# An attention stage whose key weights are stored once and sorted on the chip: one graph kernel, one change

## The chip, the cores and the metric

The kernel runs on one core of a Trainium2 chip. The core has a matrix engine (TensorE, "PE", whose weight loads the profile lists apart as "PEld"), a vector engine (VectorE, "DVE"), a scalar engine with lookup functions (ScalarE, "ACT"), a general engine (GpSimd, "POOL") and a queue processor (SyncE, "SP"), each with its own in-order list of instructions, and sixteen DMA engines between main memory (HBM) and on-chip memory (SBUF). Matrix products land in PSUM, eight banks of 512 numbers on each of 128 partitions. The metric is the device time of one execution in microseconds. Before the change it is 12,053.6 us, the median of three runs (12,050.65 to 12,054.63).

## The reference

The input is `x` (3,327 nodes by 128) and a dense matrix `adj` (3,327 by 3,327). Four layers follow each other, each of the form `x = x + layer(relu(layernorm(x)), adj)`. Only layer 0 matters here; it takes nearly all the time. It is an attention with an unusual reshape:

```
q = (x @ Wq.T).reshape(d, n, h)      # d = 128 "heads", n = 3327 nodes, h = 8 elements
k = (x @ Wk.T).reshape(d, n, h)
v = (x @ Wv.T).reshape(d, n, h)
a = einsum('dnh,dmh->dnm', q, k) * scale + adj + adj
a = softmax(a, axis=2)
out = einsum('dnm,dmh->dnh', a, v).reshape(n, h * d)
return out @ Wo.T
```

So there are 128 heads of only 8 elements, and for each of them a full 3,327 by 3,327 table of exponentials, 1.4 thousand million in all. Layers 1 to 3 multiply `adj` with a matrix of 128 columns and do work per node.

## The kernel before

**Preparing (the first 390 us).** `x` is normalized and projected. For q and for k, the projection of a pair of node tiles is split into a high part rounded to the matrix engine's fast format (`F32R`) and the remainder: ACT copies PSUM to the high part (L364), DVE subtracts it (L365), ACT squares it (L366), POOL sums the squares (L368), and SP stores both halves (L371) to `qS_d` and `kS_d` in HBM. A bound on the scores is formed from the norms. A second path (the functions `whole` and `part_of`), taken only where that bound is large, is skipped with this input.

**The main stage.** The work is cut into chunks `c` of 476 queries (7), groups `g` of four heads (32), and pairs `q` of key tiles (13); a key tile is 128 keys, spaced 13 apart. One (c, g, q) is a unit; there are 2,912, taken in that order. In a unit, for two key tiles r = 0, 1:

- `seed` (DVE, L612) copies the pair's tiles of transposed `adj` (already less a bound per query, L560) into PSUM.
- `scores` (PE, L618) adds the products of one head's k and q on top, in rows 64r to 64r+63 of the array, a separate bank for each r. The 64 rows hold the high and low parts of the new head's k and q, and of the previous head's with q negated, so that each head's table is made out of the previous head's.
- `exps` (ACT, L630) takes exp of two banks at a time, 952 numbers on each partition.
- `values` (PE, L638) multiplies them with v and a column of ones into one bank `po`, four heads in four column strips.

For a group's end `store` copies `po` (DVE, L650) and POOL issues four small stores (L654).

**Loads.** All loads of the next group are issued by SP when unit q = 1 of the present group comes up (`load_qk`): per head j and half r, two transfers of 16 rows of k into `KT` (L525) and three of q into `QS` (L527, L529), 40 in all; then two of v (L543). `KT`, `QS` and `VA` have two buffers each. `KT` holds k as it lies in HBM, so the weights of one key tile are every 13th column (`q::NQ`, 52 bytes apart). At q = 4 POOL negates q (L537), spreads v (L549) and touches the loaded tile (`all_here`, L553); the group's first score waits for that.

**Order.** All engines' orders in this stage are written out by hand: a loop over time slots `i`, four per unit, emits the exponentials of unit u and head j at slot 4u + 3j, the scores one or two slots ahead, and the values 11 and 13 slots behind. Side work is put at units by `plan(u, f)`. Between the groups a square of `adj` for the next chunk is read and turned by `plan_squares`; the maximum of its rows ("a row's bound") goes through HBM: `gather` (four stores, L299), `back` (one load into `four`, L304), `finish` (two small DVE operations, L308 and L309, and a store, L310), at 12, 16 and 20 units after the load of the second half.

**The rest (from 10,937 us).** The output product and layers 1 to 3.

Of the kernel before, what the change touches and what calls it, by code (L numbers as in the profile page):

```python
# [10 lines left out]
F32 = mybir.dt.float32  # L11
# [3 lines left out]
F32R = mybir.dt.float32r  # L15
# [7 lines left out]
P = 128  # L23
N = 3327
D = 128
H = 8
# [59 lines left out]
def gnn_kernel(ctx: ExitStack, tc: tile.TileContext, x, adj, Wq, Wk, Wv, Wo, embed, layer,  # L86
# [13 lines left out]
    qS_d = dram.tile([2, H, GP], F32, name="qS_d")  # L100
    kS_d = dram.tile([2, H, GP], F32, name="kS_d")
    oT_d = dram.tile([H + 1, GP], F32, name="oT_d")
# [226 lines left out]
    with tc.tile_pool(name="a1", bufs=1) as a1, tc.tile_pool(name="a2", bufs=2) as a2, \  # L329
# [23 lines left out]
        for t0 in range(0, NT, 2):  # L353
            for s, to in (("q", qS_d), ("k", kS_d)):
                st = {i: a2.tile([P, H, 2 * P], F32R, name=f"st_{s}{i}") for i in range(2)}
                n2 = a2.tile([P, 2, P], F32, name=f"n2{s}")
                for i in range(2):
                    t = t0 + i
                    sq = a4.tile([P, H, P], F32, name="sq")
                    for b in range(2):  # L360
                        ps = projected(s, t, b)
                        by_e = ps.rearrange("p (e i) -> p e i", e=4)
                        part = (slice(None), slice(4 * b, 4 * b + 4), slice(i * P, (i + 1) * P))
                        nc.scalar.copy(st[0][part], by_e)  # L364
                        nc.vector.tensor_tensor(st[1][part], by_e, st[0][part].bitcast(F32), op=ALU.subtract)  # L365
                        nc.scalar.activation(sq[:, 4 * b:4 * b + 4, :], by_e, AF.Square)  # L366
                    for m in (4, 2, 1):
                        nc.gpsimd.tensor_tensor(n2[:, i:i + 1, :] if m == 1 else sq[:, 0:m, :],  # L368
                                                sq[:, 0:m, :], sq[:, m:2 * m, :], op=ALU.add)
                for half in range(2):  # L370
                    nc.sync.dma_start(places(to, t0, 2, H, half * H * GP), st[half].bitcast(F32))  # L371
                nc.gpsimd.dma_start(bass.AP(tensor=n2_d[s].tensor, offset=n2_d[s].offset + t0 * P,
                                            ap=[[NT * P, P], [1, 2 * P]]), n2.rearrange("p t i -> p (t i)"))
            if t0 % 6 == 0 and len(bounds) < squares_of(0):
                bounds.append(squares(a_t, len(bounds), a1))
                bounds[-1].gather()
# [44 lines left out]
    with tc.tile_pool(name="d1", bufs=1) as d1, tc.tile_pool(name="d2", bufs=2) as d2, \  # L421
# [9 lines left out]

        def part_of(tensor, d, c0, w, name):
            return whole(tensor[:, :, 0:GN].rearrange("i e (d n) -> i e d n", n=N)[
                :, :, ds(d, 1), c0:c0 + w].rearrange("i e a n -> i e (a n)"), w, name)

        with tc.If(loose > 0):
            for s in range(squares_of(0), NT):
                squares(d2, s, d2)
            for t in range(NT):
# [3 lines left out]
                with tc.For_i(0, HEADS, 1) as d:  # L443
                    kh = part_of(kS_d, d, 0, N, "kh")
                    qh = part_of(qS_d, d, t * P, m, "qh")
                    mx = d2.tile([P, 7], F32, name="mx")
# [11 lines left out]
            for c in range(NC):  # L458
# [5 lines left out]
                with tc.For_i(0, HEADS, 1) as d:  # L464
                    kh = part_of(kS_d, d, 0, N, "kh")
                    qh = part_of(qS_d, d, c0, w, "qc")
                    mb = d2.tile([P, CW], F32, name="mb")
# [31 lines left out]
    with tc.tile_pool(name="e1", bufs=1) as e1, tc.tile_pool(name="e_adj", bufs=30) as e_adj, \  # L499
# [4 lines left out]

        KT = [e1.tile([P, 3, HALF], F32R, name=f"KT{i}") for i in range(2)]
        QS = [e1.tile([P, 4, CW], F32R, name=f"QS{i}") for i in range(2)]
        VA = [e1.tile([P, NT, 4, H + 1], F32, name=f"VA{i}") for i in range(2)]

        seen = e1.tile([P, 3], F32, name="seen")
        S = [e_ps.tile([P, 3 if i == 0 else 2, 512], F32, name=f"S{i}") for i in range(3)]  # L510
        po = e_ps.tile([P, 512], F32, name="po")

        def load_qk(c, g):

            b = (c * NG + g) % 2
            w, c0 = width_of(c), c * CW
            for j in range(4):
                d = 4 * g + j
                k0, nk = max(0, j - 1), 1 if j in (0, 3) else 2
                q_d = qS_d[:, :, d * N + c0:d * N + c0 + w].rearrange("i e n -> (i e) n")  # L520
                for r in range(2):
                    r0 = 64 * r + 32 * (1 - j % 2)
                    k_d = kS_d[:, :, d * N + r * HALF:d * N + (r + 1) * HALF].rearrange("i e n -> (i e) n")
                    for i in range(2):
                        nc.sync.dma_start(KT[b][r0 + 16 * i:r0 + 16 * i + 16, k0:k0 + nk, :].bitcast(F32),  # L525
                                          k_d.unsqueeze(1).to_broadcast([16, nk, HALF]))
                    nc.sync.dma_start(QS[b][r0:r0 + 16, j, :w].bitcast(F32), q_d)  # L527
                    for i in range(2):
                        nc.sync.dma_start(QS[b][r0 + 16 + 8 * i:r0 + 24 + 8 * i, j, :w].bitcast(F32),  # L529
                                          q_d[8 - 8 * i:16 - 8 * i])  # L530
# [20 lines left out]
        def all_here(c, g):  # L551

            return nc.gpsimd.tensor_copy(seen, KT[(c * NG + g) % 2][:, :, 0].bitcast(F32))  # L553

# [14 lines left out]
        with tc.If(loose < 1), tc.manual_schedule():  # L569
            for i in range(2):  # L570
                nc.gpsimd.memset(VA[i], 1.0)
            zero = e1.tile([32, 512], F32, name="zero")
            nc.vector.memset(zero, 0.0)
            for i in range(2):
                nc.vector.memset(QS[i][:, 0, :].bitcast(F32), 0.0)

            for bank in [s[:, i, :] for s in S for i in range(s.shape[1])] + [po]:
                nc.tensor.matmul(bank, zero[:, :P], zero, start=True, stop=True)

# [34 lines left out]
            def scores(u, j):  # L614
                c, g, q = pairs[u]
                w, b = width_of(c), (c * NG + g) % 2
                for r in range(2):
                    x = nc.tensor.matmul(  # L618
                        bank(u, r), KT[b][64 * r:64 * r + 64, max(0, j - 1), q::NQ],
                        QS[b][64 * r:64 * r + 64, j, :w], start=False, stop=True, skip_group_check=True)  # L620
                    if (j, q, r) == (0, 0, 0):
                        tc.add_manual_dep(x.ins, here.pop(c * NG + g).ins.name, after, reason="the loads")
                    touch(u, [r], x)
# [22 lines left out]
            def store(u):  # L646
                c, g, q = pairs[u]
                w = width_of(c)
                o = e2.tile([P, CW], F32, name="OS")
                nc.vector.tensor_copy(o[:, :w], po[:, :w])  # L650
# [5 lines left out]
            def loads(u):  # L656
# [3 lines left out]
                if k + 1 < NC * NG:  # L660
                    nxt = divmod(k + 1, NG)
                    if q == 1:
                        load_qk(*nxt)
                        v_of[k + 1] = load_v(*nxt)
# [19 lines left out]
            def plan_squares(c):  # L684
                for k, s in enumerate(range(squares_of(c), squares_of(c + 1))):
# [8 lines left out]
                    plan(u + 12, b.gather)  # L694
                    plan(u + 16, b.back)
                    plan(u + 20, b.finish)

            v0 = load_v(0, 0)
            load_qk(0, 0)
            shift_of[0] = load_shift(0)  # L700
            negate_q(0, 0)
            spread_v(0, 0, v0)
            here[0] = all_here(0, 0)
            adj_of[0] = [load_adj(0, t, shift_of[0]) for t in range(NT)]

# [320 lines left out]
```

## Time and profile before

| what | value |
|---|---|
| median of the runs | 12,053.6 us |
| the profiled execution | 12,062.8 us, span 12,060.9 us |
| mean granted clock of PE | 0.968 |
| main stage, first to last exponential | 389.6 to 10,937.3 us |
| PE / ACT / DVE / POOL busy in the span | 95% / 88% / 40% / 16% |
| weight loads of the scores (L618) | 23,296 of 339 ns |
| exponentials of 952 | 973 ns each |

"Busy" is the time in which at least one instruction of the engine is under way; overlapping instructions count once, and an instruction's duration includes its pipeline, so the next one may start before it ends. The idle time listed for an engine is what lay before its instructions, with the event that ended it.

### The profile page before, as it was taken

What the parts mean: (1) busy time and instruction counts of PE and PEld (TensorE: products, weight loads), DVE (VectorE), ACT (ScalarE), POOL (GpSimd) and SP (SyncE); (2) the same over time, 40 slices, a digit from 0 to 9 for tenths busy, and PEclk for the clock granted to TensorE, in tenths of its full rate; (3) what the DMA queues carried; (4) which work ended last, traced back from release to release, by engine and by line L of the source; (5) the groups of instructions that cost most, each with busy time, mean ns of one, the idle gap of its engine ahead of it and who ended that gap; (6) DMA issues with size and microseconds to landing.
All of it is one profiled execution on the core that took longest, in us unless ns stands there. A gap on an engine that the chain in (4) does not pass through costs nothing.

```text
span 12060.9 us, 195358 instructions
## 1 busy us (share of the span) xinstructions
PE 11421.9 (95%) x72798; PEld 4955.8 (41%) x72798; DVE 4807.2 (40%) x7304; ACT 10618.0 (88%) x13981; POOL 1881.1 (16%) x3162
## 2 busy tenths in 40 slices
PE   5899999999999999999999999999999999996668
PEld 2344444444444444444444444444444444444334
DVE  4344433444334433344333444334433333335335
ACT  4799999999999999999999999999999999994100
POOL 4211112111121111211112111121111211110000
PEclk8899999999999999999999999999999999997789
DMA  9655545555455444554545555455544544442456
GB/s 285 128 86 85 90 74 111 88 83 89 77 108 89 86 79 76 109 90 84 87 79 105 90 87 84 82 104 90 88 76 79 97 80 77 78 78 84 147 186 238
DMA packets 787902, 1215.46 MB, mean 101 GB/s; under 512 B 415211, under 2 KB 682348, under 8 KB 771340
## 3 DMA queue, kind: packets, MB, share of 16 engines
q1 hardware_dynamic: 745512, 1073.57, 47.8%
q0 software_dynamic: 41440, 129.30, 3.7%
q8 instruction: 588, 9.63, 0.4%
q14 instruction: 362, 2.97, 0.1%
HBM read 1069.27 MB, written 132.97 MB: 100 GB/s over the span
## 4 chain that ended last, share of the span: by engine, by line
PE 87%; DMA 6%; DVE 3%; ACT 2%; SPq 1%; issue 1%; POOL 1%; DVEq 0%; ACTq 0%; POOLq 0%
PE po L638 42%; PE S L618 40%; PE pu L822 4%; DMA QS<-qS_d 2%; DMA KT<-kS_d 1%; ACT e L630 1%; DMA strip<-adjT 1%; PE ps_t L808 1%; DMA four<-rowmax_d 1%; POOL sq L368 0%; PE ps_y L767 0%; DVE s L202 0%; ACT tmp L200 0%; DMA v_d<-st_v 0%; PE ps_t L348 0%
## 5 line engine op out<-in xcount | busy, mean ns | idle before, releaser
L630 ACT ACTIVATE e<-S 128x952 f32<-128x952 f32 (+3 forms) x13589 | 10359.3, 857 | 188.4 <-PE S L618 173.7
L612 DVE COPY S<-a 128x476 f32<-128x476 f32 (+1 forms) x5824 | 3739.8, 654 | 6233.6 <-ACT e L630 5976.6
L638 PE MATMUL po<-e,VA 128*9 128x476 f32 (+1 forms) x46592 | 5765.0, 567 | 0.0
L618 PEld LDWEIGHTS S<-QS,KT 64*128 64x128 f32 x23296 | 3744.8, 339 | 4804.7 <-ACT e L630 2344.0
L618 PE MATMUL S<-QS,KT 64*128 64x476 f32 (+1 forms) x23296 | 5495.3, 523 | 120.4 <-DVE S L612 116.1
L654 POOL DMA_DIRECT2D oT_d<-OS x896 | 470.7, 531 | 6349.2 <-DVE OS L650 6272.2
L638 PEld LDWEIGHTS po<-e,VA 128*9 128x9 f32 x46592 | 691.1, 88 | 1333.9 <-issue 1278.6
L537 POOL TENSOR_SCALAR QS<-QS 32x476 fp32r<-32x476 f32 (+1 forms) x1344 | 781.8, 582 | 1292.1 <-DMA QS<-qS_d 780.7
L124 ACT COPY uT<-pu 128x494 f32<-128x494 f32 (+2 forms) x12 | 6.3, 527 | 458.3 <-PE pu L822 457.8
L822 PE MATMUL pu<-strip,y 128*128 128x494 f32 (+2 forms) x728 | 295.6, 568 | 92.7 <-DVE y L849 92.7
L822 PE MATMUL pu<-strip,h 128*128 128x494 f32 (+2 forms) x728 | 294.6, 567 | 69.2 <-DVE h L214 66.7
L549 POOL COPY VA<-VR 128x832 f32<-128x832 f32 x224 | 198.1, 884 | 1001.7 <-DMA VR<-v_d 851.4
L560 POOL TENSOR_TENSOR a<-a,shb 128x476 f32<-128x476 f32 (+1 forms) x182 | 212.9, 1207 | 248.4 <-DMA a<-adjT 227.3
L822 PEld LDWEIGHTS pu<-strip,y 128*128 128x128 f32 (+1 forms) x728 | 139.5, 192 | 248.3 <-issue 143.4
L825 DVE TENSOR_REDUCE s<-strip 128x1 f32<-128x3327 f32 (+1 forms) x52 | 188.1, 3617 | 113.0 <-DMA strip<-adjT 62.4
L822 PEld LDWEIGHTS pu<-strip,h 128*128 128x128 f32 (+1 forms) x728 | 138.9, 191 | 224.7 <-issue 141.9
L279 DVE STREAM_TRANSPOSE cols<-rows 128x416 f32<-128x416 f32 x208 | 187.9, 912 | 15.9 <-DMA rows<-in_adj_dram 15.9
L650 DVE COPY OS<-po 128x476 f32<-128x476 f32 (+1 forms) x224 | 146.2, 653 | 91.2 <-PE po L638 86.0
L820 POOL DMA_DIRECT2D strip<-adjT x39 | 20.7, 532 | 794.2 <-PE pu L822 776.4
L124 ACT COPY hT<-pu 128x494 f32<-128x494 f32 (+1 forms) x4 | 2.2, 548 | 147.7 <-PE pu L822 147.7
L222 PE MATMUL ps_t<-ident,h 128*128 128x128 f32 x78 | 20.5, 429 | 117.3 <-DVE h L214 103.3
L128 DVE COPY uT<-pu 128x494 f32<-128x494 f32 (+2 forms) x12 | 6.8, 576 | 292.2 <-PE pu L822 291.8
(152 smaller groups left out, 1694.1 us busy)
## 6 DMA issues: line engine op xcount, KB each, us to landing
KT<-kS_d SPq DMA_DIRECT2D x1792, 208.0 KB
KT<-kS_d SPq DMA_DIRECT2D x1792, 104.0 KB
VR<-v_d SPq DMA_DIRECT2D x448, 208.0 KB
strip<-adjT POOLq DMA_DIRECT2D x39, 1663.5 KB, 8.4
strip<-adjT SPq DMA_DIRECT2D x36, 1663.5 KB
QS<-qS_d SPq DMA_DIRECT2D x3072, 14.9 KB
QS<-qS_d SPq DMA_DIRECT2D x1536, 29.8 KB
adjT<-cols SPq DMA_DIRECT2D x52, 832.0 KB
```

What stands on the lines that cost most here:

```text
L279: nc.vector.transpose(self.cols[:, :, 32 * j:32 * j + 32], self.rows[:, j, :].rearrange("p (x q) -> p q x", q=NQ))
L537: nc.gpsimd.tensor_scalar(QS[b][r0:r0 + 32, j + 1, :w], QS[b][r0:r0 + 32, j, :w].bitcast(F32), -1.0, 0.0, op0=ALU.mult, op1=ALU.add)
L549: nc.gpsimd.tensor_copy(VA[(c * NG + g) % 2][:, :, :, 0:H], v.rearrange("p j (t e) -> p t j e", e=H))
L560: nc.gpsimd.tensor_tensor(a[:, :w], a[:, :w], shift[:, :w], op=ALU.subtract)
L612: touch(u, [r], nc.vector.tensor_copy(bank(u, r), adj_of[c][2 * q + r][:, :w]))
L618: x = nc.tensor.matmul(bank(u, r), KT[b][64 * r:64 * r + 64, max(0, j - 1), q::NQ], QS[b][64 * r:64 * r + 64, j, :w], start=False, stop=Tr ...
L630: touch(u, range(a, b), nc.scalar.activation(e[:, a:b, :w], S[u % 3][:, lo + a:lo + b, :w], AF.Exp, scale=2.0))
L638: nc.tensor.matmul(po[32 * j:32 * j + H + 1, :w], VA[k % 2][:, r * NQ + q, j, :], e_of[u, j][:, at, :w], start=(q == 0 and r == 0), stop=( ...
L650: nc.vector.tensor_copy(o[:, :w], po[:, :w])
L654: nc.gpsimd.dma_start(oT_d[:, d * N + c * CW:d * N + c * CW + w], o[32 * j:32 * j + H + 1, :w])
L822: nc.tensor.matmul(pu[c][:, :w], y[:m, t, :], s[:m, c * AW:c * AW + w], start=(t == 0), stop=(t == NT - 1))
L825: nc.vector.tensor_reduce(deg[:m, t:t + 1], s[:m], axis=AX.X, op=ALU.add)
```

## The change

k is no longer split by ACT and DVE and stored as two halves. DVE copies it from PSUM as it is, and it is stored once (`k_d`). In the main stage one tile `KR` takes a group's k as it lies in HBM, in 32 transfers of 8 rows each (before: 16 transfers of 16 rows), issued at q = 3 instead of q = 1. POOL then makes the weights: for each pair q, `sort_k` reads the 3 by 128 numbers of that pair from `KR`, 52 bytes apart, once through a multiplication with a column `less` (0 or -1 by row) that writes the rounded high part negated, and once more in an addition, into `KT[:, q]`, where they lie side by side. `KR` and `KT` have one buffer each. The sorting of pair i of the next group is put at units 8 to 15 of the present one; at a chunk's last group, and for the first group, DVE does it. `all_here` touches `QS` instead of `KT`. The tile `OS` has one buffer instead of two. Of a row's bound, `back` and `finish` come 18 and 29 units after the load instead of 16 and 20.

```diff
-    kS_d = dram.tile([2, H, GP], F32, name="kS_d")
+    k_d = dram.tile([H, GP], F32, name="k_d")
...
-                        nc.scalar.copy(st[0][part], by_e)
-                        nc.vector.tensor_tensor(st[1][part], by_e, st[0][part].bitcast(F32), op=ALU.subtract)
+                        if s == "k":
+                            nc.vector.tensor_copy(st[0][part], by_e)
+                        else:
+                            nc.scalar.copy(st[0][part], by_e)
+                            nc.vector.tensor_tensor(st[1][part], by_e, st[0][part].bitcast(F32), op=ALU.subtract)
                         nc.scalar.activation(sq[:, 4 * b:4 * b + 4, :], by_e, AF.Square)
...
-                for half in range(2):
-                    nc.sync.dma_start(places(to, t0, 2, H, half * H * GP), st[half].bitcast(F32))
+                if s == "k":
+                    nc.sync.dma_start(places(k_d, t0, 2, H), st[0])
+                for half in range(2) if s == "q" else ():
+                    nc.sync.dma_start(places(qS_d, t0, 2, H, half * H * GP), st[half].bitcast(F32))
...
-        KT = [e1.tile([P, 3, HALF], F32R, name=f"KT{i}") for i in range(2)]
+        KR = e1.tile([P, 3, HALF], F32, name="KR")
+        KT = e1.tile([P, NQ, 3, P], F32R, name="KT")
+        hi = [e1.tile([P, 3, P], F32R, name=f"hi{i}") for i in range(2)]
+        less = e1.tile([P, 1], F32, name="less")
...
-        def load_qk(c, g):
+        def load_k(g):
+            for j in range(4):
+                d = 4 * g + j
+                k0, nk = max(0, j - 1), 1 if j in (0, 3) else 2
+                for r in range(2):
+                    of = k_d[:, d * N + r * HALF:d * N + (r + 1) * HALF]
+                    for i in range(4):
+                        r0 = 64 * r + 32 * (1 - j % 2) + 8 * i
+                        nc.sync.dma_start(KR[r0:r0 + 8, k0:k0 + nk, :],
+                                          of.unsqueeze(1).to_broadcast([8, nk, HALF]))
+
+        def sort_k(q, eng):
+            of = KR.rearrange("e k (p q) -> e q k p", q=NQ)[:, q]
+            h = hi[q % 2]
+            eng.tensor_scalar(h, of, less[:, 0:1], None, op0=ALU.mult)
+            eng.tensor_tensor(KT[:, q], of, h.bitcast(F32), op=ALU.add)
+
+        def load_q(c, g):
...
-                    k_d = kS_d[:, :, d * N + r * HALF:d * N + (r + 1) * HALF].rearrange("i e n -> (i e) n")
-                    for i in range(2):
-                        nc.sync.dma_start(KT[b][r0 + 16 * i:r0 + 16 * i + 16, k0:k0 + nk, :].bitcast(F32),
-                                          k_d.unsqueeze(1).to_broadcast([16, nk, HALF]))
...
-            return nc.gpsimd.tensor_copy(seen, KT[(c * NG + g) % 2][:, :, 0].bitcast(F32))
+            return nc.gpsimd.tensor_copy(seen, QS[(c * NG + g) % 2][:, :, 0].bitcast(F32))
...
-                        bank(u, r), KT[b][64 * r:64 * r + 64, max(0, j - 1), q::NQ],
+                        bank(u, r), KT[64 * r:64 * r + 64, q, max(0, j - 1), :],
...
+                    if q == 3:
+                        load_k(nxt[1])
+                        for i in range(NQ):
+                            plan(u + (5 + i // 2 if i < 10 else i), sort_k, i,
+                                 nc.vector if g == NG - 1 else nc.gpsimd)
                     if q == 1:
-                        load_qk(*nxt)
+                        load_q(*nxt)
                         v_of[k + 1] = load_v(*nxt)
...
-                    plan(u + 16, b.back)
-                    plan(u + 20, b.finish)
+                    plan(u + 18, b.back)
+                    plan(u + 29, b.finish)
...
-            load_qk(0, 0)
+            load_k(0)
+            load_q(0, 0)
...
             here[0] = all_here(0, 0)
+            for q in range(NQ):
+                sort_k(q, nc.vector)
```

## The prediction

> **What bounds the kernel now.** I read the page's totals first, then the groups of instructions, the waits, and the timelines of SP and POOL through one load of a group.
>
> ```profile
> PE 11421.9 (95%) x72798; PEld 4955.8 (41%) x72798; DVE 4807.2 (40%) x7304; ACT 10618.0 (88%) x13981; POOL 1881.1 (16%) x3162
> ...
> L618 PEld LDWEIGHTS S<-QS,KT 64*128 64x128 f32 x23296 | 3744.8, 339 | 4804.7 <-ACT e L630 2344.0 <-DVE S L612 2254.3 <-issue 203.2
> L763 PEld LDWEIGHTS ps_t<-ident,ot 128*128 128x128 f32 x208 | 24.9, 147 | 14.6 <-DVE ot L756 14.6
> L822 PEld LDWEIGHTS pu<-strip,y 128*128 128x128 f32 x700 | 134.2, 192 | 242.4 <-issue 138.0 <-DVE y L849 93.3
> ```
>
> PE and ACT go hand in hand through the main stage. In the trace, exponentials that wait for nothing start 0.860 us apart (952 wide) and 0.447 (476 wide); three units have ten of the first and four of the second, 10.39 us, so ACT alone would take 13 x 10.39 / 3 = 45.0 us per group. The groups really take 46.3: about every seventh wide exponential starts up to 0.15 us late, behind a score. And there PE loads weights that are 13 columns apart: 339 ns for 128 columns, where the contiguous 128 columns of the other two rows take 147 and 192.
>
> ```profile
> DVE b L308 <- DMA four<-rowmax_d: 144.4, 22, 8.3
> ...
> 5183.77 1.42 DVE L612 COPY S<-a 128x476 f32<-128x476 f32 x2 [2.43 <-ACT e L630]
> 5190.73 0.16 DVE L308 TENSOR_REDUCE b<-four 128x1 f32<-128x4 f32 x1 [5.55 <-DMA four<-rowmax_d]
> 5193.67 1.82 ACT L630 ACTIVATE e<-S 128x952 f32<-128x952 f32 x2 [4.17 <-PE S L618]
> ```
>
> The second loss: 22 times `finish` stands at the head of DVE's list before its load has come, the seeds queue behind it, PE waits for the seeds and ACT for PE. By the starts of the exponentials the 223 group periods sum to 10,497 us; 22 of them take 51.7 to 55.3, together 150 above 46.4 each.
>
> ```profile
> 5017.94 0.66 SPq L529 DMA_DIRECT2D QS<-qS_d  x2
> 5020.73 0.80 SPq L525 DMA_DIRECT2D KT<-kS_d  x2
> 5039.93 0.94 SPq L543 DMA_DIRECT2D VR<-v_d  x2
> ...
> 5029.43 2.10 POOL L654 DMA_DIRECT2D oT_d<-OS  x4 [29.55 <-DVE OS L650]
> 5045.87 0.19 POOL L553 COPY seen<-KT 128x3 f32<-128x3 f32 x1
> ```
>
> One group's load (group start at 5018.2): SP issues from 5016.6 to 5040.9, POOL is ready at 5046, the next group needs it at 5064. So loads have 18 us to spare, and POOL is idle most of the time. Both are what the change spends.
>
> **Contiguous weights: the gain.** Per pair of heads the trace shows 0.81 to 0.98 us of scores and 0.91 of values. Two weight loads in a row lie on that path; each shortened by 339 - 192 = 147 ns (or - 147 = 192) takes PE from 3.6 us per unit (two such pairs) to some 3.0 to 3.3, below ACT's 3.46. So inside a group ACT becomes the bound: 45.0 instead of 46.3, 223 x 1.3 = 290 us at most, and no more however fast the weights come.
>
> **The bound's steps.** `back` moves from behind the group's 42 transfers to behind the new ones, at q = 5; `finish` moves 9 units, into the next group's q = 3, some 30 us later. The `four` load needs 2.8 us (chain). DVE then waits for nothing, and the 150 us go; what is late next is the group's first score, below. The cover is the distance; if groups stretch, it stretches too.
>
> **The preparation.** k's stores fall from 26 to 13 of 1,024 KB, 13.6 MB, at the 303 GB/s of 60 to 130 us 45 us; but POOL is busy 60.6 of those 70 us with sums that stay, so I take 32. ACT loses 52 casts of 0.61 us there, DVE swaps a 0.68 subtraction for a copy: nothing, as both wait. The first group's 26 sorting operations on DVE are new, 14 to 22 us, partly beside loads of q and `adj` that set the start today (351 to 390): +10. Net -22.
>
> **The sorting: what it puts in a ring.** `KR` has one buffer, and each sorting step reads all its rows at some columns. So the next load can't start before the thirteenth step, and no step before the whole load has landed. POOL's list makes it longer: the four stores of `oT_d`, which wait for the end of the group's values, stand before the thirteenth step. Where before two buffers let a load run beside everything, the ring is now load R, twelve steps s, stores 2.10, a step s, and again R; if it is longer than ACT's 45.0 it is the group's period, because the next group's first score needs the first step. q's negation (six of 0.58), `VA` (0.88) and `seen` come behind the thirteenth step and run beside R.
>
> ```profile
> L537 POOL TENSOR_SCALAR QS<-QS 32x476 fp32r<-32x476 f32 x1152 | 670.7, 582 | 1132.9 <-DMA QS<-qS_d 694.8 <-PE S L618 240.0 <-DMA KT<-kS_d 98.8
> L368 POOL TENSOR_TENSOR sq<-sq 128x512 f32<-128x512 f32 x52 | 66.1, 1271 | 44.8 <-ACT sq L366 44.5
> L368 POOL TENSOR_TENSOR sq<-sq 128x256 f32<-128x256 f32 x52 | 37.6, 723 | 4.1
> L553 POOL COPY seen<-KT 128x3 f32<-128x3 f32 x224 | 41.9, 187 | 1.2 <-DMA QS<-qS_d 1.2
> L279 DVE STREAM_TRANSPOSE cols<-rows 128x416 f32<-128x416 f32 x208 | 187.9, 912 | 15.9 <-DMA rows<-in_adj_dram 15.9
> L287 DVE TENSOR_REDUCE rm<-rows 128x1 f32<-128x416 f32 x208 | 117.8, 575 | 0.0
> ```
>
> *The step s.* One-input operations cost 187 + 0.83 ns per number, two-input ones 175 + 2.14. For 384 numbers side by side that is 0.51 + 1.00; dependent POOL operations in the trace follow each other after 0.08, twice: s = 1.67, the low end. No POOL row reads 52 bytes apart. Others do: PE's loads (339 against 192 or 147) and DVE's turning of `rows` (912 against a reduction's 575), factors of 1.6 to 2.3. With 1.6 on what is streamed from `KR` (one of the two inputs in the addition): 0.70 + 1.24 + 0.16 = 2.1, my value, as L279 is the nearest in form. With 2.3: 0.92 + 1.53 + 0.16 = 2.6, the high end.
>
> [...]
>
> *The load R.* 384 rows of 6,656 bytes as before, but in 32 transfers of 8 rows. SP needs 0.37 for each: 11.8. Landing marks in the trace come from sixteen DMA engines for a 16-row transfer and from eight for an 8-row one. A row takes 0.42 us in the load's first transfers, 0.64 on average and 0.25 at least. If always the same eight engines serve, each moves 48 rows: 20.2 at 0.42. With 0.9 to the first row and 1.3 from the last to its mark, R = 22.4; I take it because k's rows run without q's between. Low end: engines that alternate, SP's issue sets it, 11.8 + 2.2 = 14.0. High: 48 x 0.64 + 2.2 = 33.
>
> [...]
>
> *The ring:* 22.4 + 13 x 2.1 + 2.1 + 0.4 (two hand-overs) = 52.2 us against 46.3. Ends: 14.0 + 21.7 + 2.5 = 38.2, which is under ACT's 45.0; and 33 + 33.8 + 2.5 = 69.
>
> *DVE beside a busy POOL.* From 60 to 130 us POOL is busy 87% and DVE's PSUM copies take 0.69 (L128) as elsewhere; priced at nothing. Were the seeds half as long again, DVE at 40% has the room.
>
> *The last group of six chunks.* DVE sorts there. Its first step waits at q = 8 for a load that the ring brings some 20 us later, with `adj`'s loads beside it, and the seeds queue behind: 16 to 24 us each, of which the next group, whose load can start early, returns about 7. 6 x 13 = +80.
>
> **Sum.** 12,062.8 + (223 x 52.2 - 10,497 = 1,144) - 22 + 80 = 13,265 for a profiled execution; this one lies 9 above the median of the runs, so 13,255.
>
> **Rivals.**
>
> *The ring fits (faster).* From R + 13 s below 42.5, it ends before ACT needs it, and 45.0 rules: 223 x 45.0 - 10,497 = -462, less 22, plus up to 80: 11,570 to 11,650. For it: s = 1.67 with R up to 20.8 does it, and the row's minimum of 0.25 would make R 14. Against it: it needs the low half of both terms.
>
> *The weights don't get faster.* 64-row loads are nowhere in the trace with contiguous columns. Then a ring that fits leaves 46.3 to 46.4 per group, and only the bound's 150 and 22 go: about 11,880 to 11,970. Against: every contiguous load of 128 columns in the warm stages lies near 140 to 230.
>
> *Worse than the ring.* If eight engines write to few places at once, a row keeps the 0.64 or reaches the 0.95 of the slowest twentieth; with s = 2.6 that gives 69 us and more, above 17,000.
>
> **Chances.** The ring sets the period between 47.2 and 59.5: 0.61. It is longer: 0.11. It fits, with faster weights: 0.19; without: 0.06. Within 0.2% (about what a measurement of this kernel can tell from no change): 0.03. So faster 0.25, slower 0.72. The predicted time is that of the ring, 13,255; its own range is 12,150 to 14,900 (a period of 47.2 to 59.5). The whole range must take in the ring that fits: 11,600 to 14,900, which leaves out the longest rings and the best case's edge, some 0.15.
>
> **What would show it.** PE's score loads near 150 to 200 ns. POOL's sorting 13 pairs per group, with means of 0.70 and 1.24, busy over 60%. KR's transfers starting only behind the thirteenth step, and SP's longest wait there, on POOL. ACT's idle before the first unit of each group, some 6 to 7 us, released by PE, and PE by POOL. `four` no longer waited for. I am wrong if the sorting reads at the contiguous rate, or the load lands within 20 us of its first issue: then ACT is busy through and the groups take 45.

## The result, and the profile after

The changed kernel takes 17,886.8 us (median of 4 runs, 17,852.4 to 17,904.4) against 12,054.1 before (4 runs): a ratio of 1.4836, 95% interval 1.481 to 1.4862. It is slower by about half. I had forecast slower, 13,255, with an upper end of 14,900. The sign and the mechanism hold; the size does not. The profiled execution has a span of 17,902.6 us.

The page's totals and the chain of the changed kernel:

```profile
PE 11420.1 (64%) x72798; PEld 3563.5 (20%) x72798; DVE 4992.2 (28%) x7489; ACT 10403.0 (58%) x13929; POOL 9785.6 (55%) x8805
...
DMA 40%; POOL 26%; PE 15%; ACT 9%; DVE 3%; issue 3%; SPq 3%; POOLq 0%; DVEq 0%; ACTq 0%
```

ACT and PE are about as long busy as before (10,403 and 11,420 us against 10,618 and 11,422), but in a span that is half as long again. No engine is busy for more than 64% of it. Nothing is the bound all the time; something alternates. The chain says what: two thirds of it are a DMA (36% are loads into `KR` alone) and POOL.

The waits of the changed kernel (engine and line, what it waited for: us in total, times, longest), the engines' and then those of SP's queue:

```profile
ACT e L665 <- PE S L653: 6245.9, 703, 56.4
PEld S L653 <- POOL KT L546: 6244.3, 940, 34.7
...
POOL hi L545 <- DMA QS<-qS_d: 3906.7, 137, 36.0
...
POOL hi L545 <- DMA KR<-k_d: 1075.8, 41, 35.5
```

```profile
SPq L538 <- POOL KT L546: 5680.4, 214, 36.7
```

This closes a circle. ACT waits for PE, PE for POOL's sorted weights, POOL for the load, and SP, before it issues the load, for POOL. The third line names `QS`, and a learner should not follow it: a wait for several semaphores is put down to the one that came last by the profile. The load of `KR` is what has just landed: in the median of all loads the first step starts 0.28 us behind the last landing mark of `KR`. One turn of the circle, in the timelines of SP and POOL (start, duration, engine, line, operation, count, and in brackets the idle time before):

```profile
8031.24 30.90 SPq L538 DMA_DIRECT2D KR<-k_d  x32
```

```profile
8030.01 1.21 POOL L546 TENSOR_TENSOR KT<-KR,hi 128x384 fp32r<-128x384 f32 x1
8031.31 3.89 POOL L567 TENSOR_SCALAR QS<-QS 32x476 fp32r<-32x476 f32 x6
...
8036.08 0.18 POOL L583 COPY seen<-QS 128x4 f32<-128x4 f32 x1
8066.24 1.58 POOL L545 TENSOR_SCALAR hi<-KR,less 128x384 fp32r<-128x384 f32 x1 [29.98 <-DMA QS<-qS_d]
8067.90 1.18 POOL L546 TENSOR_TENSOR KT<-KR,hi 128x384 fp32r<-128x384 f32 x1
8069.06 1.60 POOL L545 TENSOR_SCALAR hi<-KR,less 128x384 fp32r<-128x384 f32 x1
```

The thirteenth step ends at 8031.22 and the load's first transfer starts at 8031.24. The last row lands at 8065.97 and the first step of the next group starts at 8066.24. ACT meanwhile stands still for 27.6 us:

```profile
8024.14 18.42 ACT L665 ACTIVATE e<-S 128x952 f32<-128x952 f32 x24
8070.11 1.88 ACT L665 ACTIVATE e<-S 128x952 f32<-128x952 f32 x3 [27.55 <-PE S L653]
```

Over 216 such turns the median is: R (first issue to first step) 34.6, the thirteen steps with the four stores of `oT_d` among them 39.5, then 0.03 to the next issue; a whole turn takes 74.2 us. The groups, by the starts of the exponentials, have a median of 74.4, against 46.3 before. What the ring is made of stands in the groups of instructions:

```profile
L545 POOL TENSOR_SCALAR hi<-KR,less 128x384 fp32r<-128x384 f32 x2821 | 4540.3, 1609 | 6155.0 <-DMA QS<-qS_d 3906.7
...
L653 PEld LDWEIGHTS S<-QS,KT 64*128 64x128 f32 x23296 | 2353.0, 196 | 11488.0 <-POOL KT L546 6244.3
L546 POOL TENSOR_TENSOR KT<-KR,hi 128x384 fp32r<-128x384 f32 x2821 | 3387.3, 1201 | 235.4
```

The weights load in 196 ns instead of 339, as the change means them to. The addition is where I had it (1.24 forecast, 1.20 measured). The multiplication takes 1.61 us, and I had 0.70.

So the prediction leaves two questions. Why is a step 2.88 us long and not 2.1? And why does a load take 34.6 us and not 22.4? Beside these: are the two gains (weights, the bound's steps) as large as I put them, and can they be had without the ring? The theory for the experiments is that the period of a group is R plus the steps whenever that sum is over ACT's 45. Its rival is that a busy POOL, or a slower PE clock (0.804 granted instead of 0.968), costs the other engines something of itself.

### The profile page after: what moved, and what is told of

It is laid out like the page before. It is cut to its first block, busy times and chain, and to the rows that moved or that the text cites. A ratio compares the mean times of both kernels' runs of the same rounds, so it can differ in the third digit from the quotient of the medians.

```text
span 17902.6 us, 209205 instructions
## 1 busy us (share of the span) xinstructions
PE 11420.1 (64%) x72798; PEld 3563.5 (20%) x72798; DVE 4992.2 (28%) x7489; ACT 10403.0 (58%) x13929; POOL 9785.6 (55%) x8805
## 4 chain that ended last, share of the span: by engine, by line
DMA 40%; POOL 26%; PE 15%; ACT 9%; DVE 3%; issue 3%; SPq 3%; POOLq 0%; DVEq 0%; ACTq 0%
DMA KR<-k_d 36%; POOL hi L545 13%; POOL KT L546 10%; ACT e L665 9%; PE po L673 6%; PE S L653 6%; PE pu L865 2%; SPq L538 2%; DMA QS<-qS_d 2%; POOL oT_d L689 2%; DVE S L647 1%; DMA rows<-in_adj_dram 1%; DVE KT L546 0%; PE ps_t L851 0%; DVE hi L545 0%
## 5 line engine op out<-in xcount | busy, mean ns | idle before, releaser
L665 ACT ACTIVATE e<-S 128x952 f32<-128x952 f32 (+3 forms) x13589 | 10169.2, 906 | 6247.5 <-PE S L653 6245.9
L653 PE MATMUL S<-QS,KT 64*128 64x476 f32 (+1 forms) x23296 | 5195.6, 463 | 5992.6 <-POOL KT L546 4895.9
L545 POOL TENSOR_SCALAR hi<-KR,less 128x384 fp32r<-128x384 f32 x2821 | 4540.3, 1609 | 6155.0 <-DMA QS<-qS_d 3906.7
L673 PE MATMUL po<-e,VA 128*9 128x476 f32 (+1 forms) x46592 | 6057.8, 593 | 11.1 <-DVE OS L685 4.2
L653 PEld LDWEIGHTS S<-QS,KT 64*128 64x128 f32 x23296 | 2353.0, 196 | 11488.0 <-POOL KT L546 6244.3
L546 POOL TENSOR_TENSOR KT<-KR,hi 128x384 fp32r<-128x384 f32 x2821 | 3387.3, 1201 | 235.4
L579 POOL COPY VA<-VR 128x832 f32<-128x832 f32 x224 | 200.0, 893 | 22.4 <-DMA VR<-v_d 8.3
L545 DVE TENSOR_SCALAR hi<-KR,less 128x384 fp32r<-128x384 f32 x91 | 95.4, 1049 | 332.1 <-DMA a<-adjT 256.7
## 6 DMA issues: line engine op xcount, KB each, us to landing
QS<-qS_d SPq DMA_DIRECT2D x1536, 29.8 KB
```

The costliest lines, as they stand in the source:

```text
L545: eng.tensor_scalar(h, of, less[:, 0:1], None, op0=ALU.mult)
L546: eng.tensor_tensor(KT[:, q], of, h.bitcast(F32), op=ALU.add)
L579: nc.gpsimd.tensor_copy(VA[(c * NG + g) % 2][:, :, :, 0:H], v.rearrange("p j (t e) -> p t j e", e=H))
L653: x = nc.tensor.matmul(bank(u, r), KT[64 * r:64 * r + 64, q, max(0, j - 1), :], QS[b][64 * r:64 * r + 64, j, :w], start=False, stop=True, ...
L665: touch(u, range(a, b), nc.scalar.activation(e[:, a:b, :w], S[u % 3][:, lo + a:lo + b, :w], AF.Exp, scale=2.0))
L673: nc.tensor.matmul(po[32 * j:32 * j + H + 1, :w], VA[k % 2][:, r * NQ + q, j, :], e_of[u, j][:, at, :w], start=(q == 0 and r == 0), stop=( ...
```

## Experiments

Beside the experiments the kernel before took 12,025 to 12,052 us (medians), so times of different experiments can be compared to within some 30 us. Where no number of runs is given, a time is that of one run.

### The gains, each alone

**weights_side**: the kernel before, whose weights are read side by side from the unsorted tile.

```
-  bank(u, r), KT[b][64 * r:64 * r + 64, max(0, j - 1), q::NQ],
+  bank(u, r), KT[b][64 * r:64 * r + 64, max(0, j - 1), q * P:(q + 1) * P],
```

> The kernel before with one edit: the score weights are read from 128 neighbouring columns of KT instead of every 13th, so the keys of a tile are the wrong ones; loads, buffers and all other work are unchanged, and nothing is sorted. Theory: the weight loads fall from 339 to about 196 ns as in the changed kernel, PE drops under ACT, the groups take 45.0 instead of 46.3 us, and the time falls by about 290 us to 11,765. Rival, the weight loads were hidden behind other PE work and ACT's waits have another cause: 12,050 us.

Measured: 11,764.6 us, where the kernel before, run beside it, took 12,026.2: 262 us less. By the starts of the exponentials the group periods sum to 10,213 us against 10,497 in the profile of before, 284 less. (That the time falls on the forecast 11,765 is luck: the forecast went from 12,054.) The median group takes 45.12 us, and the weight loads, in the groups of this kernel,

```profile
L618 PEld LDWEIGHTS S<-QS,KT 64*128 64x128 f32 x23296 | 2281.1, 185 | 5507.8 <-DVE S L612 2790.7
```

185 ns instead of 339. ACT is then the bound inside the groups, at the 45.0 that I had worked out of its starts.

**bound_steps**: the kernel before, with the steps of the bound further apart.

```
-  plan(u + 16, b.back)
-  plan(u + 20, b.finish)
+  plan(u + 18, b.back)
+  plan(u + 29, b.finish)
```

> The kernel before with only the bound's steps moved (18 and 29 units behind the load instead of 16 and 20). My account of before: 22 long groups hold 150 us in which DVE waits for `four`. If the distance is all that they need: 12,054 - 150 = 11,900, no group period above 49 in the trace (the last groups of the six chunks apart) and no 5.5 us waits of DVE for `four`. Rival: something else is late next in these groups (the rows' transposes, the seeds): 11,980 to 12,050.

Measured: 11,901.0 us (4 runs) against 12,052.4 beside it, ratio 0.9877, interval 0.986 to 0.9893. The group periods sum to 10,348 us against 10,497 before, none is above 48 where 22 were, and the wait of DVE for `four` (144.4 us before) is no longer among the waits. Nothing else became late in its place.

### What a step costs

**sort_unit_stride**: the changed kernel, sorting 384 numbers that lie side by side.

```
-  of = KR.rearrange("e k (p q) -> e q k p", q=NQ)[:, q]
+  of = KR[:, :, q * P:(q + 1) * P]
```

> The changed kernel, but each sorting step reads 128 neighbouring columns of KR instead of every 13th, so the keys of a tile are the wrong ones; the work is the same. Theory (ring: load R, thirteen sorting steps s, four stores; in the changed kernel 35.0 + 13 x 2.85 + 2.3 = 74.4 us, the median of its group periods): if the 52-byte step is what makes a step dear, the multiplication falls from 1.60 to about 0.51 us, the addition from 1.20 to about 1.00, s to 1.7, the period to 35 + 22 + 2.3 = 59 us, and the time by 223 x 15 to about 14,500 us. Rival 1, the column operand of the multiplication is dear and not the step: the multiplication stays near 1.6, s near 2.7, about 17,400 us. Rival 2, the load alone sets the period and the sorting hides in it: about 17,890 us whatever s is.

**sort_immediate**: the changed kernel, with a constant in place of the column `less`.

```
-  eng.tensor_scalar(h, of, less[:, 0:1], None, op0=ALU.mult)
+  eng.tensor_scalar(h, of, -1.0, 0.0, op0=ALU.mult, op1=ALU.add)
```

> The changed kernel, but the multiplication takes the constant -1 in place of the column of 0 and -1, so the split into high and low parts is wrong on half the rows; the reads keep their 52-byte step. If the step is dear: the multiplication stays at 1.6 us and the time at about 17,890 us. If the column operand is dear: the multiplication falls to about 0.7, s to 2.0, the period to 62.7 us and the time to about 15,300 us.

**sort_both**: both edits.

> The changed kernel with both changes to the sorting step at once: reads of 384 numbers side by side, and a constant in place of the column operand (it sorts wrong keys, and no row keeps its rounded value). If the two costs add: multiplication 1.61 - 0.73 - 0.37 = 0.51, addition 1.00, a step 1.67, which is the low end of my prediction; 13 steps and the stores 24, with R 33 a ring of 57 to 58 and a time of 14,200 to 14,500. If they overlap (the slower of two rates rules): multiplication near 0.7 to 0.9, a ring of 60 and over, 14,700 or more.

Measured, with the page's means and the ring's medians:

| kernel | time | multiplication | addition | from step to step | steps with stores | R | turn of the ring |
|---|---|---|---|---|---|---|---|
| changed kernel | 17,886.8 | 1.609 | 1.201 | 2.88 | 39.5 | 34.6 | 74.2 |
| sort_unit_stride | 16,197.3 | 1.244 | 1.004 | 2.31 | 32.2 | 33.7 | 66.1 |
| sort_immediate | 15,747.4 | 0.876 | 1.200 | 2.13 | 29.8 | 33.1 | 63.2 |
| sort_both | 14,048.6 | 0.513 | 1.004 | 1.57 | 22.5 | 33.7 | 56.4 |

The groups of sort_both:

```profile
L546 POOL TENSOR_TENSOR KT<-KR,hi 128x384 fp32r<-128x384 f32 x2821 | 2832.4, 1004 | 235.1
L545 POOL TENSOR_SCALAR hi<-KR 128x384 fp32r<-128x384 f32 x2821 | 1447.1, 513 | 6016.7 <-DMA QS<-qS_d 3434.3 <-DMA KR<-k_d 1406.9 <-DMA rows<-in_adj_dram 545.6
```

Four corners of a square, and the costs add. The column operand in place of constants costs POOL 1.244 - 0.513 = 0.731 us beside contiguous reads and 1.609 - 0.876 = 0.733 beside reads 52 bytes apart. The step of 52 bytes costs 0.365 on the multiplication (1.609 - 1.244; 0.363 the other way round) and 0.197 on the addition, where one of two inputs has it. Without both, the two operations are at 0.513 and 1.004: exactly the low end that the prediction had from `QS` and `sq`. Neither pure theory of the first run held, since both edits bite. The edit to constants also gives the instruction a second operation (an addition of 0), which the form with the column does not have; that the column and not this difference is dear was not tested apart.

### What a load costs

**k_twice**: the changed kernel, k stored twice (unsplit), so that a transfer has 16 rows.

```
+  for half in range(2):
+      nc.sync.dma_start(places(k_d, t0, 2, H, half * H * GP), st[0])
...
-  for i in range(4):
-      r0 = 64 * r + 32 * (1 - j % 2) + 8 * i
-      nc.sync.dma_start(KR[r0:r0 + 8, k0:k0 + nk, :], of.unsqueeze(1).to_broadcast([8, nk, HALF]))
+  for i in range(2):
+      r0 = 64 * r + 32 * (1 - j % 2) + 16 * i
+      nc.sync.dma_start(KR[r0:r0 + 16, k0:k0 + nk, :], of.unsqueeze(1).to_broadcast([16, nk, HALF]))
```

> The changed kernel, but k is stored twice, one copy behind the other, and KR is loaded by 16 transfers of 16 rows instead of 32 of 8; same bytes into KR, sorting unchanged. Theory (an 8-row transfer runs on eight of sixteen DMA engines, and a row costs 0.54 to 0.76 us on its engine): R falls from 35.0 to about 18 us, the period to 18 + 37 + 2.3 = 57.4 and the time to about 14,100 us. Rival, the rows are held back by something all engines share (they come at 70 to 99 GB/s now): R stays near 35 and the time near 17,900 us.

Measured: 15,319.2 us; R 21.8, steps 39.5, a turn of 61.3. The steps have not moved; R is shorter by 12.8 and the turn by 12.9. With the sorting variants, which moved the steps and not R, the period is shown to be the sum of the two. But R did not halve with twice the engines, so I looked at when each transfer's last row landed.

Between the last landing marks of one transfer and of the next (medians over the loads of 217 groups; "one range": the transfers of a group's first and last head, which write one of three key ranges; "two ranges": those of the two middle heads, which write the same rows into two):

```
kernel             engines   one range        two ranges
changed kernel     8         0.60 / 0.48 us   1.52 us
k_twice            16        0.76 / 0.70      1.72
```

(The two figures of one range are those of the first and of the last head. "Engines" are counted by landing marks: in the traces of before and of the changed kernel a transfer of 16 rows leaves sixteen, one of 8 rows eight. While nothing but rows of `KR` moves, from 8048 to 8060 in the changed kernel, the share of the sixteen DMA engines is 0.52.) A transfer to two ranges has twice the bytes but takes about two and a half to three times as long.

**k_split**: the changed kernel with one transfer for each range, back to back.

```
-  nc.sync.dma_start(KR[r0:r0 + 8, k0:k0 + nk, :], of.unsqueeze(1).to_broadcast([8, nk, HALF]))
+  for k in range(k0, k0 + nk):
+      nc.sync.dma_start(KR[r0:r0 + 8, k, :], of)
```

> The changed kernel, with each transfer of 8 rows to two key ranges (two copies of the same 6,656 bytes) split into two transfers of one key range, 48 in place of 32. In the changed kernel a transfer to one range landed every 0.54 us, one to two ranges every 1.51 (0.755 per row of each DMA engine). If the double transfer is the dear form, R falls to 48 x 0.54 + 1.5 = 27.5 and the time by 223 x 7 to 16,300. If rows cost the same in any form and the difference comes from what else moves at that time (q's rows, v), R stays near 34.6 and the time near 17,890.

Measured: 17,779.7 us, R 33.6. The form is not it: the middle heads' transfers now land every 0.61 to 0.77 us, the outer heads' every 0.57 and 0.47.

**k_order**: the same 48 transfers, all rows of one range before the other range.

```
-  for i in range(4):
-      r0 = 64 * r + 32 * (1 - j % 2) + 8 * i
-      for k in range(k0, k0 + nk):
+  for k in range(k0, k0 + nk):
+      for i in range(4):
+          r0 = 64 * r + 32 * (1 - j % 2) + 8 * i
           nc.sync.dma_start(KR[r0:r0 + 8, k, :], of)
```

> The changed kernel with single-range transfers (48, as before this run), but ordered so that all rows of one key range go first and then all of the other, in place of the two copies of the same rows back to back. With the copies back to back the two middle heads' rows landed every 0.755 us on an engine, the outer heads' every 0.49 to 0.54. If writing one partition's two ranges one after the other is what costs: all rows at 0.54, R = 48 x 0.54 + 1.5 = 27.5 and the time near 16,300. If it is something else of the two middle heads' rows (their places in memory, or that they are read eight times), R stays at 33.6 and the time near 17,780.

Measured: 16,336.4 us, R 26.0, a turn of 65.8. All rows land every 0.47 to 0.59 us now. SP's timeline of one load in k_split, and then of one in k_order:

```profile
7604.90 31.06 SPq L539 DMA_DIRECT2D KR<-k_d  x48
```

```profile
6959.78 18.35 SPq L539 DMA_DIRECT2D KR<-k_d  x48
```

18.35 us for 48 transfers instead of 31.06. Both lines are of the same group of heads and queries, but this load of k_order is among its shortest: in the median SP takes 22.2 us for a load there and 29.8 in k_split, and R, from the first issue to the first step, is the 26.0 against 33.6. The sequence of sources is the same in both, since all eight transfers of a half of a head read the same rows; so are the bytes and the engines. Only the order of the destinations differs. Two copies written to the same partitions one behind the other are what made the middle heads dear (one run of each kernel, 217 loads in each). Why a DMA engine is slower at that, these runs do not show.

### Both gains without the ring

**one_copy_pool**: k is split and stored twice as before, and each pair is put side by side by one copy. There is still one raw tile, so the ring is there, but it is short.

```
 (before.py, with)
+  KR = e1.tile([P, 3, HALF], F32R, name="KR")
+  KT = e1.tile([P, NQ, 3, P], F32R, name="KT")
...
+  nc.sync.dma_start(KR[r0:r0 + 16, k0:k0 + nk, :].bitcast(F32), of.unsqueeze(1).to_broadcast([16, nk, HALF]))
...
+  def sort_k(q, eng):
+      of = KR.rearrange("e k (p q) -> e q k p", q=NQ)[:, q]
+      eng.tensor_copy(KT[:, q], of.bitcast(F32))
...
+  plan(u + (5 + i // 2 if i < 10 else i), sort_k, i, nc.vector if g == NG - 1 else nc.gpsimd)
...
+  plan(u + 18, b.back)
+  plan(u + 29, b.finish)
```

> k stays stored twice, split in the preparation as before; its rows land in one raw tile by 16-row transfers, and POOL (DVE in the last group of a chunk) puts each pair's 384 numbers side by side with one copy; the bound's steps as in the changed kernel. The ring is then a load of some 22 us (as with k stored twice), 13 steps and 2.1 of stores. A copy by the measured rows: 0.51 for 384 numbers side by side plus 0.37 for the 52-byte step = 0.88, so 13 x 0.96 = 12.5 and a ring of 37 us, shorter than ACT's 45.1. If the ring decides only where it is longer than ACT's work, the kernel runs at the weights' pace without the bound's waits: 11,765 - 150 = 11,615, plus up to 6 x 20 for the last groups: 11,610 to 11,740. Rival: the busy POOL or the sorting itself costs the other engines something beyond the ring: above 11,800. If copies are as dear as the multiplication by a column was (1.61): 22 + 22 + 2 = 46, near 11,850.

Measured: 11,704.5 us (4 runs), ratio 0.9712, interval 0.9696 to 0.9728: faster than both kernels. Totals, chain and the copy in its page:

```profile
PE 10976.2 (94%) x72798; PEld 3491.9 (30%) x72798; DVE 4882.2 (42%) x7395; ACT 10356.3 (88%) x13981; POOL 4237.1 (36%) x5983
...
ACT 79%; PE 7%; issue 6%; DMA 4%; DVE 3%; SPq 1%; POOL 0%; DVEq 0%; POOLq 0%; ACTq 0%
...
L527 POOL CAST KT<-KR 128x384 fp32r<-128x384 f32 x2821 | 2332.0, 880 | 3766.5 <-DMA KR<-kS_d 2756.8
```

The copy takes 0.880, as priced. A load takes 21.8, and copies that follow each other start 0.81 us apart. Load, copies and stores so need 21.8 + 12 x 0.81 + 0.88 + 2.11 = 34.5 us, less than ACT's 45: POOL waits behind its twelfth copy, with the stores and the thirteenth still to come, for the end of the group's values (2,010 us in all, before L665). The ring's turn is therefore 45.1, and the median group 45.12, as in weights_side. POOL is busy for 36% (16% before) and DVE's seeds of 476 still take 655 ns, so the rival that a busy POOL costs the others something is out at this level of use. What is left above the floor are the six last groups of a chunk, 60 to 62 us each, together 99 above the ordinary. In DVE's timeline of one:

```profile
4732.99 1.42 DVE L623 COPY S<-a 128x476 f32<-128x476 f32 x2 [2.07 <-ACT e L641]
4749.23 1.90 DVE L527 CAST KT<-KR 128x384 fp32r<-128x384 f32 x2 [14.82 <-DMA a<-adjT]
4751.06 1.40 DVE L623 COPY S<-a 128x476 f32<-128x476 f32 x2
```

DVE's first copy stands 14.8 us at the head of its list, with the seeds behind it. (Again the name in brackets is only the last semaphore; the load of `KR`, issued at 4726.3, is what landed then.)

### The last groups

**last_on_pool** (on the changed kernel) and **one_copy_last** (on one_copy_pool): POOL sorts in the last group too.

```
-  nc.vector if g == NG - 1 else nc.gpsimd)
+  nc.gpsimd)
```

> The changed kernel, with POOL sorting in the last group of a chunk too. In the changed kernel these six groups took 106 to 113 us, of which 6 to 27 come back in the next group: net +80 to +150 over 12 ordinary periods of 74.4. If DVE's wait at the head of its list is the cause, these pairs of groups fall to ordinary ones, 17,890 - 100 = 17,790 or lower. Rival: POOL's 26 sums of adjacency tiles (1.3 us each, 33 us) then stand in the ring of these groups, and the pair takes as long or up to 6 x 33 more: 17,890 to 18,090.

Measured: 18,010.5 us. The rival: the group pairs now lie 215 us above ordinary ones together, where they had 76 in the changed kernel.

> The kernel with k stored twice and one copy per pair on POOL, with POOL also in the last group of a chunk. There DVE's first copy waited 14.8 us for the load with the seeds behind it, and the six groups took 61 to 62 us in place of 45.1, together about 95 to 100. If that wait is all: 11,704 - 97 = 11,607. Rival: POOL has 26 sums of 1.28 us, six negations and the rest in the same group, 54 us of work against 45, and the copies come late in its list: 11,650 to 11,800.

Measured: 11,739.7 us (4 runs), ratio 0.9763, interval 0.9747 to 0.978 (one_copy_pool: 0.9696 to 0.9728), slower than one_copy_pool. The last groups take 65.6 to 66.1 us. The rival again: POOL's 26 sums of `adj` tiles stand among its copies, and the copies come late.

**one_copy_later**: one_copy_pool with three edits for those groups.

```
+  for k in range(k0, k0 + nk):
+      for i in range(2):
+          nc.sync.dma_start(KR[r0:r0 + 16, k, :].bitcast(F32), of)
...
-  plan(u + (5 + i // 2 if i < 10 else i), sort_k, ...)
+  plan(u + (5 + i // 2 if i < 10 else i) + (2 if g == NG - 1 else 0), sort_k, ...)
...
-  while len(adj_of[c + 1]) < min(NT, 2 * q + 6):
+  while q >= 3 and len(adj_of[c + 1]) < min(NT, 2 * q + 2):
```

> The kernel with k stored twice and one copy per pair, with three changes for the last group of a chunk: rows of one key range before the other (24 transfers of 16 rows in place of 16 with two copies each), the adjacency tiles of the next chunk from the fourth pair on instead of from the first, so that POOL's last copies don't stand behind sums that wait for them, and DVE's copies two units later. The six last groups took 61 to 62 us, 99 together above 45.1 each with the group behind. If the late load and DVE's wait for it cause that, the copies are done in time and most of it goes: 11,605 to 11,660. If another thing holds them (26 loads of adjacency tiles in one group, the seeds), near 11,704, or above where the adjacency tiles now come too late.

Measured: 11,750.5 us (4 runs), ratio 0.9772, interval 0.9755 to 0.9788. The last groups fell from 60 to 62 us to 50 to 52, but the groups behind them rose from 46 to 64 to 66, and the kernel is slower than one_copy_pool. DVE's and SP's timelines of a group behind (it starts at 3297.0) show why:

```profile
3308.70 1.52 DVE L527 CAST KT<-KR 128x384 fp32r<-128x384 f32 x1
3310.33 1.45 DVE L623 COPY S<-a 128x476 f32<-128x476 f32 x2
3329.89 0.50 DVE L527 CAST KT<-KR 128x384 fp32r<-128x384 f32 x1 [18.11 <-DMA KR<-kS_d]
```

```profile
3310.25 13.86 SPq L523 DMA_DIRECT2D KR<-kS_d  x24
```

Two units later is too late. Counted from the unit u at which the copies are planned, `load_k` of the next group comes at u + 13, and the last two copies, now at u + 13 and u + 14, stand behind it in the order that is written out. So they wait for that load, 16.8 to 18.3 us in each of the six groups, with the seeds behind them on DVE, and they copy the next group's keys in place of their own. This run leaves out the right order of two copies and does not tell what copies that are later, but still before the load, would bring. Less six such waits it would lie near 11,645, an estimate; no run shows it. A second raw tile, which would open the ring, was not tried. R alone did fall, from 21.8 to 19.6, by the order of the ranges.

## Why the prediction was wrong, step by step

**The bound of before and its two losses: right.** Weights: 290 us at most by the prediction, 284 by the group periods of weights_side and 262 by its time against the kernel before beside it. The bound's steps: 150 forecast, 151 in bound_steps.

**The preparation: right as far as this can be read.** -22 forecast; the main stage starts at 370.7 instead of 389.6, so -19. But in weights_side, bound_steps and one_copy_pool, which prepare as before, it starts at 381 to 386, so the gain is some 10 to 19. Its parts (32 of stores, 10 of sorting) were not measured apart.

**The ring: the mechanism right.** Its order (load, twelve steps, stores, a step, and again), its hand-overs and what releases whom are what the trace shows, and three kinds of change to its terms moved the period by as much. Two terms were mis-sized:

- *The step s: 2.1 forecast (low 1.67, high 2.6), 2.88 measured.* The low end was exact as a base. The part for reads 52 bytes apart was 0.19 + 0.24 = 0.43 forecast by the factor 1.6, and 0.37 + 0.20 = 0.56 measured; a small miss, and luck in part, since the factor compared two different operations (a transposition and a reduction). The large one is the column operand, `less[:, 0:1]`: 0.73 us, to which the prediction gave no price at all. The row that it took for the multiplication, the negation of `QS`, has constants there. This form was in no row of before and needed bounds of its own; with the high end built on the 52-byte step alone, the truth lay outside. Thirteen times 0.73 is 9.5 of the ring's 22 us of error.
- *The load R: 22.4 forecast (low 14.0, high 33), 34.6 measured.* That eight engines move 48 rows each was right, as far as the eight landing marks of a transfer and the DMA share of 0.52 show it. The price of a row was not: 0.42 us came from the load's first transfers, which go to one range, and stood for the 32 of 48 that go to two, which took 0.76 each (1.52 for two). The trace of before had these too, behind its average of 0.64: there the packets of a load's first transfers took 0.41 us (median), those in the middle of the load 0.77. "k's rows run without q's between" was the reason for taking the low figure, and it was not the reason for the high ones; k_order shows that the order of destinations was (R 26.0 against 33.6 in k_split). That is 12.2 us of the error.

Together 34.6 + 39.5 against 22.4 + 29.4 + 0.4 is 74.1 to 52.2, or 21.9 us in a group. By the whole stage: the 223 group periods sum to 16,366 us; forecast were 10,497 + 1,144 + 80 = 11,721; the difference of 4,645 and 3 of the preparation are the 4,639 by which the profiled execution (17,904.4) differs from the forecast one (13,265), to within 9.

**DVE beside a busy POOL: right.** The seeds of 476 take 655 ns, as before, at a POOL that is busy 55% of the span. The other way round there is a price that nobody named: POOL's operations on `adj` tiles of 476 (the sums above) take 1.21 us before, and 1.36 in the changed kernel, where DVE sorts beside them; in last_on_pool, where it does not, 1.23.

**The last group of six chunks: the sum right, its parts not.** +80 forecast, +76 measured over ordinary groups; that is luck. The last groups were 31 to 39 us longer (16 to 24 forecast), and the groups behind gave back 17 to 26 (7 forecast). And that DVE sorts there is no loss against POOL: last_on_pool is slower.

**The rivals.** "Worse than the ring" came true: its 69 us and more, above 17,000, was 74.2 and 17,887. Its reason for slow rows, engines that write to few places at once, was not shown as such; k_order showed that the order of the destinations counts (a row every 0.47 to 0.59 us instead of every 0.61 to 0.77 in k_split). Its step of 2.6 had no column in it either. I had given a ring above 59.5 a chance of 0.11, as if its parts had to come together by chance. "The ring fits" is what one_copy_pool then was, by other means, at 11,704 (11,570 to 11,650 forecast for the changed kernel).

**What would show it.** Weights near 150 to 200 ns: 196. `KR`'s transfers only behind the thirteenth step, SP's longest waits there on POOL, ACT released by PE and PE by POOL: all so. Mean of the multiplication 0.70: 1.61. ACT idle 6 to 7 us before a group: 28. POOL busy over 60%: 55%, in a longer span.

## What to carry to other kernels

When a change makes one buffer do the work of two, write down the ring that it closes and add up its terms; a period is their sum, however idle every engine looks. Each term then needs a price from a row of the very same form, operands and destinations included: an operand that is a column and not a constant is another form (0.73 us more here), and so is a transfer that writes one partition twice (1.52 us for two rows here, where a row to one range took 0.48 to 0.60). And an operation that is moved to a later place in a hand-written order must still stand before the load that refills its tile. Where a cheap gain (contiguous weights, 284 us) can be had by one plain copy in idle time, it need not be joined to a saving in stores that was worth 19 at most.

## What was not expected of the hardware

- POOL's `tensor_scalar` with a column operand takes 0.73 us more than with constants on 384 numbers for 128 partitions, 1.9 ns for each number, in both kinds of reads (1.244 against 0.513 contiguous, 1.609 against 0.876 with steps of 52 bytes). On DVE the same operand costs little (0.603 against 0.543 us, both contiguous, in sort_unit_stride and sort_both), but the step of 52 bytes costs DVE more than POOL: 1.049 (changed kernel) against 0.603, or 0.45 us where POOL pays 0.365.
- Rows of 6,656 bytes that are written to one range of partitions after the other land every 0.47 to 0.59 us on eight engines (k_order); two copies back to back to the same partitions, every 0.61 to 0.77 (k_split).
- Sixteen engines are not twice as fast as eight at this: a row of each takes 0.74 us (one_copy_later, ordered) where eight take 0.50 (k_order), so that R is 19.6 against 26.0.
- In these runs the granted clock of PE is lower the less PE is busy: 0.968 at 95% (before), 0.888 at 80% (sort_both), 0.804 at 64% (the changed kernel). It explains none of the loss: inside a group the units of the changed kernel take 3.52, 3.49 and 3.39 us (medians of three kinds), ACT's pace, and just as long in one_copy_pool at 0.969.
